# A one-core GNN layer: two batches' h kept on chip, sums of blocks reordered, and where the first gate operands lie

## The chip, the core and the metric

The kernel runs on one core of a Trainium2 chip. A core has five engines that run at the same time and meet only at semaphores: TensorE (PE) for matrix products, VectorE (DVE) and GpSimd (POOL) for elementwise work, ScalarE (ACT) for activations and copies, and SyncE (SP), which here only issues transfers. Each engine takes its instructions strictly in the order of its own queue. SBUF is the on-chip memory (128 partitions), PSUM the eight banks that matmuls write, HBM the memory outside. The metric is the device time of one launch in microseconds (us). The kernel before has a median of 1826.45 us over 3 runs (1825.56 to 1828.58).

## The reference, cut to what matters

There are 32 batches of 512 nodes with 256 features, all in float32. The steps that matter:

```python
h   = relu(layernorm(x))
c   = relu(bn1(conv1x1(h)))                     # then a convolution over 17 neighbouring nodes
x_conv = relu(bn2(conv17(c)) + h)
s   = h @ w_se.T + b_se                         # 3 numbers per node
A   = exp(-|s_i - s_j|^2) * adj                 # 512 x 512 per batch
msg = relu(h @ w_msg.T + b_msg)
x_nmp = A @ msg
gi  = [x_conv, x_nmp] @ w_ih.T + b_ih           # GRU gates, three of 256 each
gh  = h @ w_hh.T + b_hh
r, z = sigmoid(gi_r + gh_r), sigmoid(gi_z + gh_z)
n   = tanh(gi_n + r * gh_n)
out = x + (1 - z) * n + z * h
```

## The kernel before, in words

The batches are worked in two groups of 16 (g = 0 and g = 1), each group in two stages, and a last stage makes the gates for all 32. In time the stages are: first part of group 0 (0 to 157 us of the profile), node loop of group 0 (157 to 446), first part of group 1 (446 to 563), node loop of group 1 (563 to 853), gates of 16 pairs of batches (853 to 1825).

**First part** (`first_part`, L881 to L993). For each batch x is normalised, transposed to h with features on the partitions (tile `hT`, two buffers), stored to HBM (`hd`), put through the 1x1 convolution, and taken to the frequency domain in windows of nodes (tile `xf`). The 17-tap convolution is a product per frequency there. `conv1` (L318) drops its batch's `hT` at its end (L331), except for the last batch of a group. Near the end the first part prepares the node loop: `by_chunks` (L424) copies an `hT` into another order of nodes (tile `hq`, two buffers), and `load_h` (L413) brings back an h from HBM.

**Node loop** (`nodes`, L1036). Its order of batches is the list `todo`: the group's last batch, then the others from the first on. Each turn i works on several batches at once: `message` (PE, then DVE and ACT) of batch i+2 from its `hq`, `factors` and `exponents` of batch i+1 (small transposes on PE, copied out by ACT as `sl` and `sr`, then the products `pd` and the exponentials A), `turn` and `masked` of batch i+1 (DVE transposes the adjacency block and multiplies), and the aggregation A @ msg of batch i. Between these lie the frequency products `multiply(u)` (`product`, L372): unit u has three complex-product terms, the third of which needs `wsum` and `both`, sums that POOL makes two units ahead (`prepare`, L362). 36 units in group 0 (40 in group 1) are spread over the turns, two or three in each.

The aggregation of most batches is done with seven products of half size instead of eight (`aggregate7`, L529). It needs sums of blocks of msg (`ms`) and of A (`ts`), four of each, some of them in place. POOL makes them one turn ahead (`message_sums` L508, `affinity_sums` L499). The last two batches of group 1 are aggregated plainly (`aggregate`, L517). In `aggregate7` ACT copies each finished product out of PSUM (L545 to L553), DVE adds (L554 to L560), and `save_nmp` (L562) stores the result to HBM from ACT's queue. The result tile `nmp` has one buffer.

What orders the work is the program text: the stages run under a manual schedule, so every engine's queue follows the order of the calls. Tiles come from pools; a pool that opens later lies over the memory of one that has closed, and the first writer of a tile waits until the last user of what lay there is done. The pool `nodes` holds adj, msg, A, ts, ms and p7; `first` and `sums` lie over it in the first part of group 1; `sw`, `ops` and `late` in the gate stage.

**Gates** (the block with `load_pair(0)`, from L1164). For each pair of batches there are three operand tiles (`hp`, `np`, `cp`, for h, the aggregation and the convolution), four blocks each, with four more blocks made by POOL (`sums`, L640). The gate products follow the same seven-product scheme, with combined weights in one tile `sw` (seven slices; `load_combined` loads slices 0 and 1 first, the others later). `load_pair(0)` and both weight loads are issued from POOL's queue, so they lie in line with POOL's sums. `gates_rz` (L672) uses the slices in the order 0, 1, 2 and on.

Of the kernel before, what the change touches and what calls it, by code (L numbers as in the profile page):

```python
# [11 lines left out]
FP = mybir.dt.float32  # L12
AF = mybir.ActivationFunctionType
ALU = mybir.AluOpType

P = 128
# [49 lines left out]
def gnn_layer(  # L66
# [251 lines left out]
    def conv1(b):  # L318
        H1[b] = pools["first"].tile([P, NC, D], FP, tag="h1", name=f"h1_{b}", bufs=2)
        h = N // D  # L320
        for c0 in range(0, NC, h):
            p = bank(f"pc1_{b}_{c0}").rearrange("p (c d) -> p c d", d=D)
            for j in range(h):
                c = c0 + j
                for ic in range(DC):
                    nc.tensor.matmul(p[:, j, :], HT[b][:, ic, c * P : (c + 1) * P], w1[:, ic, :],  # L326
                                     start=(ic == 0), stop=(ic == DC - 1))
            h1 = H1[b][:, c0 : c0 + h, :]
            nc.vector.tensor_add(h1, p, shift1_row[:, None, :].to_broadcast([P, h, D]))
            nc.scalar.activation(h1, h1, AF.Relu)  # L330
        if b % GB != GB - 1:  # L331
            del HT[b]

    def windows_to_freq(b, xf):
# [89 lines left out]
    def by_chunks(b):  # L424
        HQ[b] = work.tile([P, DC, N], FP, tag="hq", name=f"hq_{b}", bufs=2)
        for ic in range(DC):
            nc.scalar.copy(chunks(HQ[b][:, ic, :]), by_chunk(HT[b][:, ic, :]))  # L427
        del HT[b]
# [69 lines left out]

    def affinity_sums(b):  # L499
        b11, b12, b21, b22 = quads(A[b], H)  # L500
        t = TS[b] = pools["nodes"].tile([P, 3, 2, H], FP, tag="ts", name=f"ts_{b}", bufs=1)
        sub = ALU.subtract
        nc.gpsimd.tensor_tensor(t[:, 0], b22, b12, op=sub)
        nc.gpsimd.tensor_tensor(b12, b12, b11, op=sub)
        nc.gpsimd.tensor_tensor(t[:, 1], b22, b12, op=sub)
        nc.gpsimd.tensor_tensor(t[:, 2], b21, t[:, 1], op=sub)

    def message_sums(b):  # L508
        a11, a21, a12, a22 = quads(MSG[b], P)
        t = MS[b] = pools["nodes"].tile([P, 3, 2, P], FP, tag="ms", name=f"ms_{b}", bufs=1)  # L510
        sub = ALU.subtract
        nc.gpsimd.tensor_tensor(t[:, 0], a11, a21, op=sub)
        nc.gpsimd.tensor_tensor(a21, a21, a22, op=ALU.add)
        nc.gpsimd.tensor_tensor(t[:, 1], a21, a11, op=sub)
        nc.gpsimd.tensor_tensor(t[:, 2], a12, t[:, 1], op=sub)

    def aggregate(b, dcs=range(2)):  # L517
        if 0 in dcs:
# [10 lines left out]
    def aggregate7(b):  # L529

        m11, s1, m12, m22 = quads(MSG.pop(b), P)
        b11, t1, b21, b22 = quads(A.pop(b), H)
        (s3, s2, s4), (t3, t2, t4) = ([t[:, n] for n in range(3)] for t in (MS.pop(b), TS.pop(b)))
        nmp = NMP[b] = work.tile([P, DC, N], FP, tag="nmp", name=f"nmp_{b}", bufs=1)
        c11, c12, c21, c22 = (nmp[:, i, H * j : H * (j + 1)] for i in range(2) for j in range(2))
        p1 = pools["nodes"].tile([P, H], FP, tag="p7", name=f"p7_{b}", bufs=2)

        def add_product(bk, left, right, first):
            for k in range(2):
                nc.tensor.matmul(bk, left[:, k, :], right[:, k, :], start=(first and k == 0), stop=(k == 1),  # L540
                                 skip_group_check=True)

        x, y, z = (bank(f"pn{k}_{b}")[:, :H] for k in range(3))
        add_product(x, m11, b11, True)
        nc.scalar.copy(p1, x)  # L545
        add_product(y, s2, t2, True)
        nc.scalar.copy(c12, y)
        add_product(z, s1, t1, True)
        nc.scalar.copy(c21, z)
        add_product(x, m12, b21, False)  # L550
        nc.scalar.copy(c11, x)
        add_product(y, s3, t3, False)
        nc.scalar.copy(c22, y)  # L553
        nc.vector.tensor_add(c12, c12, p1)  # L554
        nc.vector.tensor_add(c22, c22, p1)
        nc.vector.tensor_add(c22, c22, c21)
        add_product(z, s4, b22, False)
# [323 lines left out]
    def first_part(g, freq, between, left=()):  # L881
# [39 lines left out]
        for b in range(b0, b1):  # L921
# [18 lines left out]
            if g == 0:  # L940
# [11 lines left out]
                if b == b0 + 2:  # L952
                    slot()
                if b == b1 - 1:
                    load_h(b0)
                if b + 2 < b1:
                    statistics(b + 2)
# [21 lines left out]
            one, two = between(b - b0)  # L979
            conv1(b)  # L980
            if b == b1 - 1:
                load_h(b0)
            for step in one:
                step()
# [2 lines left out]
                step()  # L987
        if g > 0:
            by_chunks(b1 - 1)
            load_h(b0 + 1)  # L990
        windows_to_freq(b1 - 1, xf)
        by_chunks(b0)
        return xf  # L993

    @contextmanager
# [6 lines left out]
    with tc.tile_pool(name="freq", bufs=1) as fpool:  # L1002
# [33 lines left out]
        def nodes(g, xf, units, last, following=()):  # L1036
# [26 lines left out]
            load_h(todo[3])  # L1063
            message(todo[0])
            features(todo[0])
            message_sums(todo[0])
            message(todo[1], [0])
            factors(todo[0])
            message(todo[1], [1])
# [8 lines left out]
            affinity_sums(todo[0])  # L1078
            for i, b in enumerate(todo):
                mine = spread(units, i, last) if i < last else []  # L1080
                more = todo[i + 1 : i + 5]
# [52 lines left out]
        with phase("pw", "ahead"):  # L1134
            with phase("nodes"):
                with tc.manual_schedule():
                    nodes(0, xf, range(UNITS - LEFT), GB, range(UNITS - LEFT, UNITS - LEFT + 2))
            with phase("first", "sums"):
# [20 lines left out]
            with phase("nodes"):  # L1159
# [5 lines left out]
    with phase("late"), phase("sw"), phase("ops", bufs=2), phase("work"), tc.manual_schedule():  # L1165
# [72 lines left out]
```

## Time and profile before

| stage (us of the span) | length | PE busy | DVE busy | ACT busy | POOL busy | mean DMA |
|---|---|---|---|---|---|---|
| 0 to 220 | 220.0 | 211.3 | 165.4 | 117.5 | 89.3 | 265 GB/s |
| 245 to 440 | 195.0 | 190.8 | 164.8 | 88.3 | 157.8 | 215 GB/s |
| 440 to 560 | 120.0 | 119.1 | 98.5 | 47.9 | 44.5 | 232 GB/s |
| 590 to 810 | 220.0 | 220.0 | 172.5 | 100.2 | 168.7 | 236 GB/s |
| 840 to 880 | 40.0 | 36.3 | 8.1 | 10.2 | 29.6 | 257 GB/s |
| 905 to 1745 | 840.0 | 840.0 | 498.4 | 193.3 | 224.3 | 92 GB/s |

The table is from the view of busy time by stage. PE is busy nearly everywhere, so time can be lost in two ways only: in gaps between its instructions, and in instructions that take longer than their like elsewhere. Both are seen in the timeline of PE, where each row is a run of equal instructions with its start, its length, and in brackets the idle time before it and what ended it.

### The profile page before, as it was taken

Reading aid. Unit: us, or ns where it says so; the run is one execution under the profiler, and the core shown is the slowest. Engines: PE = TensorE matmul, PEld = TensorE weight load, DVE = VectorE, ACT = ScalarE, POOL = GpSimd, SP = SyncE. Lnnn points to the kernel's source line nnn. Section 1 sums busy time; section 2 is a strip of 40 time slices with the busy share of each in tenths; the row PEclk is TensorE's granted clock in tenths of the full one; section 3 lists DMA queues with packets and bytes.
Section 4 is the critical chain, followed back from the end, with each engine's and each line's share of the span. In section 5 each row is a group of like instructions: output and inputs, shape, how many; then the busy total and the mean of one; then the engine's idle time right before and its main releaser. Section 6 shows DMA issues by size and latency. Waiting matters only on the chain.

```text
span 1825.0 us, 21270 instructions
## 1 busy us (share of the span) xinstructions
PE 1796.4 (98%) x6974; PEld 1152.0 (63%) x6974; DVE 1236.8 (68%) x2370; ACT 621.9 (34%) x1252; POOL 782.6 (43%) x731
## 2 busy tenths in 40 slices
PE   9999999998999999999999999999999999999998
PEld 6776888887898888886445554555445554555444
DVE  7885788886896787884266556664666466645666
ACT  4555454442345454443212221222212221222121
POOL 3432688777433877776321232223221323133221
PEclk9999999999999999999999999999999999999999
DMA  9989888865669887879142244224422443234412
GB/s 260 309 291 233 234 231 224 238 208 179 214 225 224 250 241 224 244 210 287 50 117 70 57 121 121 87 35 121 121 87 41 116 121 100 54 89 121 116 22 53
DMA packets 308657, 289.32 MB, mean 159 GB/s; under 512 B 148076, under 2 KB 238732, under 8 KB 308164
## 3 DMA queue, kind: packets, MB, share of 16 engines
q1 hardware_dynamic: 282964, 225.79, 46.4%
q10 hardware_dynamic: 18992, 38.68, 6.1%
q0 software_dynamic: 6592, 23.50, 4.1%
q8 instruction: 55, 0.90, 0.2%
q14 instruction: 54, 0.44, 0.1%
HBM read 191.50 MB, written 96.40 MB: 158 GB/s over the span
## 4 chain that ended last, share of the span: by engine, by line
PE 71%; POOL 1%; issue 1%; DMA 1%; DVE 1%; ACT 0%; DVEq 0%; POOLq 0%; ACTq 0%
PE pg L666 29%; PE pn L666 15%; PE py L390 6%; PE pn L540 5%; PE pc L654 5%; PE pm L442 3%; PE pc L326 3%; PE px L341 2%; PE phT L310 1%; PE pd L486 1%; PE pz L666 1%; DMA sw<-ws 1%; DMA nd<-nmp 0%; PE psr L468 0%; POOL hp L644 0%
## 5 line engine op out<-in xcount | busy, mean ns | idle before, releaser
L644 POOL TENSOR_TENSOR hp<-hp 128x512 f32<-128x512 f32 x64 | 80.4, 1267 | 413.6 <-DMA hp<-hd 293.0
L666 PE MATMUL pg<-cp,sw 128*128 128x512 f32 x434 | 223.0, 595 | 2.2 <-DMA sw<-ws 2.2
L666 PE MATMUL pg<-hp,sw 128*128 128x512 f32 x434 | 222.7, 595 | 0.7 <-DVE rz L685 0.5
L666 PE MATMUL pg<-np,sw 128*128 128x512 f32 x434 | 222.6, 594 | 0.6 <-DMA sw<-ws 0.6
L644 POOL TENSOR_TENSOR cp<-cp 128x512 f32<-128x512 f32 x64 | 80.4, 1268 | 227.0 <-ACT cp L660 225.7
L681 ACT ACTIVATE rz<-rz,brz 128x512 f32<-128x512 f32 x93 | 67.0, 721 | 260.2 <-DVE rz L685 260.2
L390 PE MATMUL py<-wt,xf 128*128 128x256 f32 x640 | 154.2, 384 | 0.0
L666 PEld LDWEIGHTS pg<-cp,sw 128*128 128x128 f32 x434 | 82.9, 191 | 106.9 <-issue 103.6
L666 PEld LDWEIGHTS pg<-np,sw 128*128 128x128 f32 x434 | 82.7, 191 | 105.3 <-issue 103.9
L666 PEld LDWEIGHTS pg<-hp,sw 128*128 128x128 f32 x434 | 82.5, 191 | 105.5 <-issue 98.8
L357 POOL TENSOR_TENSOR wsum<-wt 128x512 f32<-128x512 f32 x78 | 105.0, 1347 | 102.1 <-DMA wt<-wd 62.3
L390 PEld LDWEIGHTS py<-wt,xf 128*128 128x128 f32 x640 | 117.1, 190 | 34.9 <-issue 20.5
L805 ACT ACTIVATE nt<-nt,vech 128x512 f32<-128x512 f32 x64 | 46.2, 722 | 236.5 <-DVE nt L804 236.5
L442 PE MATMUL pm<-wmsg,hq 128*128 128x259 f32 x512 | 117.8, 382 | 3.8 <-ACT hq L427 3.8
L326 PE MATMUL pc<-w,hT 128*128 128x256 f32 x512 | 117.9, 383 | 0.8 <-DVE hT L314 0.8
L492 DVE TENSOR_TENSOR A<-A,at 128x512 f32<-128x512 f32 x128 | 109.9, 896 | 6.8 <-ACT A L488 6.8
L666 PE MATMUL pn<-hp,sw 128*128 128x512 f32 x224 | 114.4, 592 | 0.0
L666 PE MATMUL pn<-cp,sw 128*128 128x512 f32 x224 | 114.4, 592 | 0.0
L666 PE MATMUL pn<-np,sw 128*128 128x512 f32 x224 | 114.4, 592 | 0.0
L326 PEld LDWEIGHTS pc<-w,hT 128*128 128x128 f32 x512 | 94.6, 190 | 24.0 <-issue 6.4
L442 PEld LDWEIGHTS pm<-wmsg,hq 128*128 128x128 f32 x512 | 96.3, 189 | 19.4 <-ACT hq L427 4.8
L654 PEld LDWEIGHTS pc<-back,yt 128*128 128x128 f32 x640 | 92.7, 190 | 7.7 <-issue 7.7
(169 smaller groups left out, 3422.0 us busy)
## 6 DMA issues: line engine op xcount, KB each, us to landing
wt<-wd SPq DMA_DIRECT2D x160, 256.0 KB, 5.3
adj<-in_adj_dram SPq DMA_DIRECT2D x128, 256.0 KB, 6.9
wd<-wst SPq DMA_DIRECT2D x64, 320.0 KB, 5.7
yd<-y ACTq DMA_DIRECT2D x80, 256.0 KB, 4.5
yt<-yd SPq DMA_DIRECT2D x30, 640.0 KB, 7.5
hd<-hT SPq DMA_DIRECT2D x32, 512.0 KB, 5.0
nd<-nmp ACTq DMA_DIRECT2D x32, 512.0 KB, 4.8
xb<-in_x_dram SPq DMA_DIRECT2D x128, 128.0 KB, 3.8
```

Of the source, the lines that this page charges most:

```text
L326: nc.tensor.matmul(p[:, j, :], HT[b][:, ic, c * P : (c + 1) * P], w1[:, ic, :], start=(ic == 0), stop=(ic == DC - 1))
L341: nc.tensor.matmul(p[:, j * 2 * L : (j + 1) * 2 * L], H1[b][:, c0 + j, ic * P : (ic + 1) * P], fwd, start=True, stop=True)
L357: nc.gpsimd.tensor_tensor(t, WT[g, u][:, 0], WT[g, u][:, 1], op=ALU.add)
L390: nc.tensor.matmul(dst, v[:, ic, :], w[:, ic, :], start=(ic == 0), stop=(ic == DC - 1))
L442: nc.tensor.matmul(p[:, : D + NS], hq[:, ic, c * P : (c + 1) * P], wmsg[:, ic, :], start=(ic == 0), stop=(ic == DC - 1))
L492: nc.vector.tensor_mul(A[b][:, mc, :], A[b][:, mc, :], AT.pop((b, mc)))
L540: nc.tensor.matmul(bk, left[:, k, :], right[:, k, :], start=(first and k == 0), stop=(k == 1), skip_group_check=True)
L644: nc.gpsimd.tensor_tensor(t[:, dst, :], t[:, a, :], t[:, b, :], op=sub)
L654: nc.tensor.matmul(bk[:, t0:t1], YT[p][j][:, c, oc * P : (oc + 1) * P], back[:, n : n + t1 - t0], start=(c == 0), stop=(c == len(spans) - ...
L666: nc.tensor.matmul(bk[:, t], sw[:, k, q, o, :], terms[k][q][:, t], start=(first and i == 0), stop=(i == len(ks) - 1), skip_group_check=True)
L681: nc.scalar.activation(rz[:, g, j, :], src, AF.Sigmoid, bias=brz[:, g : g + 1], scale=1.0)
L805: nc.scalar.activation(n, n, AF.Tanh, bias=b_in[:, i : i + 1], scale=1.0)
```

## The change

It has several parts.

- The h of a group's last *two* batches stays on chip: `conv1` keeps their `hT`, `by_chunks` of the last but one is done in the last turn of the first part, and `todo` begins with both. One `load_h` from HBM (512 KB) at the head of each node loop falls away, and the copy that went with it.
- In a turn, `by_chunks` for a later batch moves from before the aggregation to behind it, and the store of the aggregated batch is issued at once behind it, no longer with the next turn's first stores. On ACT's queue the store now stands ahead of the copies `sl` and `sr` of the next turn.
- The block sums of msg and A are interleaved in the order in which the products use them, and in `aggregate7` the product of s1 and t1 comes second instead of third.
- In group 0's last turn the third frequency unit moves from before the aggregation to behind it.
- `ts`, `ms` and `p7` (three buffers instead of two) get a pool of their own, `seven`, which lies in front of `nodes`. In the gate stage the tile `np` of the first pair then lies over those tiles; before, it lay over `adj`.
- The load of weight slices 2 to 6 is issued before the sums of the first `np` instead of behind them.

The purpose is to take waits out at the stage boundaries. No arithmetic is added or removed.

```diff
@@ conv1
-        if b % GB != GB - 1:
+        if b % GB < GB - 2:
             del HT[b]
@@ affinity_sums, message_sums
-        t = TS[b] = pools["nodes"].tile([P, 3, 2, H], FP, tag="ts", name=f"ts_{b}", bufs=1)
+        t = TS[b] = pools["seven"].tile([P, 3, 2, H], FP, tag="ts", name=f"ts_{b}", bufs=1)
...
+    def block_sums(b):
+        m, a = message_sums(b), affinity_sums(b)
+        for step in (*m[:2], *a[:2], m[2], a[2], m[3], a[3]):
+            step()
@@ aggregate7
-        p1 = pools["nodes"].tile([P, H], FP, tag="p7", name=f"p7_{b}", bufs=2)
+        p1 = pools["seven"].tile([P, H], FP, tag="p7", name=f"p7_{b}", bufs=3)
...
         nc.scalar.copy(p1, x)
+        add_product(z, s1, t1, True)
+        nc.scalar.copy(c21, z)
         add_product(y, s2, t2, True)
         nc.scalar.copy(c12, y)
-        add_product(z, s1, t1, True)
-        nc.scalar.copy(c21, z)
@@ first_part, last batch of a group (both groups)
+                    by_chunks(b - 1)
                     load_h(b0)
...
                     by_chunks(b)
-                    load_h(b0 + 1)
...
         windows_to_freq(b1 - 1, xf)
-        by_chunks(b0)
@@ nodes
-            todo = [b1 - 1] + list(range(g * GB, b1 - 1))
+            todo = [b1 - 1, b1 - 2] + list(range(g * GB, b1 - 2))
...
                     exponents(more[0])
-                    if len(more) > 2:
-                        by_chunks(more[2])
                     masked(more[0], [0, 1])
-                for u in mine[1:2] if more else mine[1:]:
+                for u in mine[1:2]:
                     multiply(u)
...
                 flush()
-                stores.append(partial(save_nmp, b))
+                if len(more) > 2:
+                    by_chunks(more[2])
+                save_nmp(b)
                 if more and i + 1 <= last:
-                    message_sums(more[0])
-                    affinity_sums(more[0])
-                if more:
-                    for u in mine[2:]:
-                        multiply(u)
+                    block_sums(more[0])
+                for u in mine[2:]:
+                    multiply(u)
@@ pools of both node loops
-            with phase("nodes"):
+            with phase("seven", "nodes"):
@@ head of the gate stage
         sums(HP[0], True)
+        load_combined(sw, 2, 7)
         sums(NP[0], False)
-        load_combined(sw, 2, 7)
```

More of the change, by code (lines that the diff above doesn't have):

```diff
@@ L500, in affinity_sums @@
         b11, b12, b21, b22 = quads(A[b], H)
-        t = TS[b] = pools["nodes"].tile([P, 3, 2, H], FP, tag="ts", name=f"ts_{b}", bufs=1)
+        t = TS[b] = pools["seven"].tile([P, 3, 2, H], FP, tag="ts", name=f"ts_{b}", bufs=1)
         sub = ALU.subtract
[L503 to L506, printed above, removed]
+        return [partial(nc.gpsimd.tensor_tensor, dst, x, y, op=sub)
+                for dst, x, y in ((t[:, 0], b22, b12), (b12, b12, b11), (t[:, 1], b22, b12), (t[:, 2], b21, t[:, 1]))]
     def message_sums(b):
         a11, a21, a12, a22 = quads(MSG[b], P)
-        t = MS[b] = pools["nodes"].tile([P, 3, 2, P], FP, tag="ms", name=f"ms_{b}", bufs=1)
+        t = MS[b] = pools["seven"].tile([P, 3, 2, P], FP, tag="ms", name=f"ms_{b}", bufs=1)
         sub = ALU.subtract
[L512 to L515, printed above, removed]
+        return [partial(nc.gpsimd.tensor_tensor, dst, x, y, op=op)
+                for dst, x, y, op in ((t[:, 0], a11, a21, sub), (a21, a21, a22, ALU.add),
+                                      (t[:, 1], a21, a11, sub), (t[:, 2], a12, t[:, 1], sub))]
+    def block_sums(b):
+        m, a = message_sums(b), affinity_sums(b)
+        for step in (*m[:2], *a[:2], m[2], a[2], m[3], a[3]):
+            step()
     def aggregate(b, dcs=range(2)):
@@ L981, in first_part @@
             if b == b1 - 1:
+                by_chunks(b - 1)
                 load_h(b0)
@@ L989, in first_part @@
             by_chunks(b1 - 1)
-            load_h(b0 + 1)
         windows_to_freq(b1 - 1, xf)
-        by_chunks(b0)
         return xf
@@ L1065, in nodes @@
             features(todo[0])
-            message_sums(todo[0])
+            for step in message_sums(todo[0]):
+                step()
             message(todo[1], [0])
@@ L1077, in nodes @@
             prepare(pw, g, units[1], xf)
-            affinity_sums(todo[0])
+            for step in affinity_sums(todo[0]):
+                step()
             for i, b in enumerate(todo):
@@ L1158, in gnn_layer @@
                     xf = first_part(1, freq_tile, between, left)
-            with phase("nodes"):
+            with phase("seven", "nodes"):
                 with tc.manual_schedule():
```

## The prediction

> **What bounds the kernel now.** I read the page first, then the waits of PE, then PE's timeline around each wait, and last the queues of the engine that ended it. The page says that PE has no room left but its gaps:
>
> ```profile
> PE 1796.4 (98%) x6974; PEld 1152.0 (63%) x6974; DVE 1236.8 (68%) x2370; ACT 621.9 (34%) x1252; POOL 782.6 (43%) x731
> ```
>
> The span is 1825.0 us, so PE sits idle for 28.6. PE's waits, longest total first (total, times, longest):
>
> ```profile
> PE py L390 <- POOL both L370: 4.4, 2, 4.2
> PE pm L442 <- ACT hq L427: 3.8, 2, 1.9
> PE pg L666 <- DMA sw<-ws: 2.8, 2, 2.2
> PE pn L540 <- ACT p L545: 2.8, 1, 2.8
> ```
>
> Each long one sits at a stage boundary. The node loops between them (590 to 810: PE 220.0 of 220.0) and the gates (905 to 1745: 840.0 of 840.0) have no gap, so a change there buys nothing unless it adds a wait. PE's timeline, start of the first node loop:
>
> ```profile
> 180.17 1.03 PE L540 MATMUL pn<-A,msg 128*128 128x256 f32 x4
> 183.96 2.07 PE L540 MATMUL pn<-A,msg 128*128 128x256 f32 x4 [2.77 <-ACT p L545]
> ```
>
> The like group takes 1.03 before the gap and 2.07 after it: a gap also slows what follows. ACT's timeline shows why p was late; it stood in line behind a copy that waited for a load:
>
> ```profile
> 181.95 1.14 ACT L427 COPY hq<-hT 128x512 f32<-128x512 f32 x2 [3.02 <-DMA hT<-hd]
> 183.54 0.37 ACT L545 COPY p<-pn 128x256 f32<-128x256 f32 x1
> ```
>
> End of that loop, PE and then POOL:
>
> ```profile
> 430.74 1.89 PE L390 MATMUL py<-wt,xf 128*128 128x256 f32 x8
> 436.82 2.08 PE L390 MATMUL py<-wsum,both 128*128 128x256 f32 x4 [4.19 <-POOL both L370]
> 446.39 1.64 PE L310 MATMUL phT<-ident,xn 128*128 128x128 f32 x8 [0.93 <-DVE xn L302]
> ...
> 436.04 0.72 POOL L370 TENSOR_TENSOR both<-xf 128x256 f32<-128x256 f32 x1
> ```
>
> Start of the gates, PE and then POOL:
>
> ```profile
> 869.21 1.02 PE L666 MATMUL pg<-hp,sw 128*128 128x512 f32 x2
> 874.16 2.07 PE L666 MATMUL pg<-cp,sw 128*128 128x512 f32 x2 [2.21 <-DMA sw<-ws]
> ...
> 847.68 1.47 POOL L621 DMA_DIRECT2D np<-nd  x2 [16.45 <-DVE at L475]
> 861.07 1.61 POOL L608 DMA_DIRECT2D sw<-ws  x3
> ```
>
> POOL's queue is held for 16.45 us by the np load, which waits until adj, below it in memory, has been read. Everything behind it on POOL (sums of hp and np, then the second half of sw) starts late.
>
> Last, ACT around the batch before the last, for the wait that the change adds:
>
> ```profile
> 412.75 0.59 ACT L470 COPY sr<-psr 128x512 f32<-128x512 f32 x1 [0.17 <-PE psr L468]
> 416.12 0.33 ACTq L563 DMA_DIRECT2D nd<-nmp  x1
> ```
>
> **What the Trainium skill says.** "TensorE: Matmul & The Clock Gate", section "What's actually happening": the PE clock is halved after an idle window of about 3.4 us and comes back after as much steady work, and the window runs freely. The trace agrees on the halving (granted clock 0.55, 0.50 and 0.81 in the three stretches of 3 us from 873 on), but here gaps of 0.59 and 2.21 with one slow group between them are enough. "SBUF — State Buffer", section "Who interferes with whom": a DVE instruction with two SBUF inputs contends with GpSimd's reads. The trace agrees: L555 takes 0.42 at 835.15 with POOL idle, 0.96 at 413.55 beside POOL's sums. "DMA: Bandwidth & Descriptors", section "Queues, rings and completion order": each DMA engine goes round between the queues with work. From 840 to 843.7 two queues share the engines (SP's 0.93 MB, ACT's 0.52 MB), which fits.
>
> **The change part by part.**
>
> *Start of group 0's loop.* The seven products run from 178.44 to 189.12, 10.68 us; the same 28 instructions take 6.04 in the chain of waits elsewhere: 4.64 lost. With the copy of hq moved behind L553 on ACT, p no longer waits for the load, and this wait is gone. The dropped load takes 512 KB off a saturated stretch (DMA share 0.97 to 1.24 from 156 to 183): at about 240 GB/s 2.1 us. adj of the first batch now lies over memory that PE leaves before 157, so DVE starts its transposes up to 3 us earlier than at 168.53, frees the PSUM banks of pm earlier, and the group pd at 173.52 (2.30 long against 1.14) may regain 1.2. Against it stands the next turn: POOL's sums start at 191.2, since wsum waits for a wt load issued at 182.91. If PE comes 5 us earlier, the sums must too; of the 8.7 us of sums the interleaved order has those of the second and third product ready 4.3 and 6.5 us after the start. By the 2 to 3 us that the loads come earlier this just holds. I take 5.0, from 3.0 to 5.8. The wait of 1.9 for hq (168.01, and 574.24 in group 1) stays: that copy is still queued behind the same four exponents. In group 1 no wait of the first kind exists: 0.
>
> *End of group 0's loop.* From 430.74 to the next unit's product at 447.88 PE takes 17.14. Its work there: 12 product instructions 2.59 + aggregation 6.04 + transposes 0.87 = 9.50. So 7.64 are lost. With the aggregation first, POOL's sums (429.56 to 434.9) are in time: the second product needs its in-place sum, the fourth of eight from 426.12, by 431.6, ready about 430.5; the third needs the sixth, ready 432.6, a wait of 0.2. `both` is there at 436.76, when the seven products end. Gain 7.4. The x load of group 1's second batch now waits for p7 (until 437) instead of starting at 432.60; its statistics come on DVE some 6 us later, so it costs nothing.
>
> *A new wait, one turn earlier.* The store of nmp now stands ahead of sl and sr on ACT, and waits for DVE's last add L560 (415.64 + 0.41 = 416.05). Queued behind it: sl, sr, two y copies, exponents; for sr waits PE's pd. In usual turns pd comes 6.7 us after the aggregation (257.90 to 264.64), and sr would be ready 4.5 after it: the store 3.3 behind (261.21), its issue 0.33, then sl and sr back to back 0.8 (168.34 to 169.13). No cost. In the turn before the last there is no message work, and pd follows after 3.1 us, at 415.24. sr would be ready at 416.12 + 0.33 + 0.8 = 417.3: a gap of 2.1. pd itself was stretched to 1.66 by banks that are free then, so 1.6 net, plus some half-clock: 2.0, from 0.5 to 4.5. Net gain of this end: 7.4 - 2.0 = 5.4 (3 to 7).
>
> *Head of the gates.* np now lies over ms, ts and p7, which L560 releases at 836.9. POOL then issues np at 837.0 and the first part of sw to about 840, does the hp sums (4 x 1.27 = 5.2) to 845.3, and issues the rest of sw at about 845.3 instead of 861.07. The transfers from 826 on are 14.64 MB; at the 360 GB/s of full stretches 40.7 us, and the late ones (np of pair 1 and x, 2.1 MB) are behind, so sw lands near 862, before PE needs it at 869. From 869.21 to 880.65 PE does six products that elsewhere take 36.05 / 42 = 0.858 each: 11.44 - 5.15 = 6.29 regained. Against it: the earlier np and sw join the store of nd at 837.10, on which ACT waits 6.15 and through it the last aggregation (PE gaps 0.50 and 0.41 at 845.62 and 848.01). A third queue on the engines makes its transfer 1 to 1.5 us longer: minus 1.1 (0 to 3). Net 5.2 (3 to 6.3).
>
> *The rest at nothing.* The order of products and sums in the steady turns: POOL is done 3 us before PE asks (810.72 against 813.68). The later hq copy: on ACT it would end near 257.9, 3 us before its products at 261.04. The third p buffer: no wait for it seen. The copy of the last-but-one batch in the first part: ACT has gaps of 1.6 and 1.1 us there, and is 40% busy.
>
> Sum: 5.0 + 5.4 + 5.2 = 15.6. 1826.45 - 15.6 = 1810.9.
>
> **The rivals.**
> - *All gaps close, no new wait:* 5.8 + 7.4 + 6.3 + 0.9 (the two small gaps) = 20.4, 1806. For it: the new waits hang on DVE and DMA timing of a few tenths. Against it: L560 at 416.05 is plain in the trace. 0.13.
> - *One boundary stays as it is* because loads bind there: the start of the first loop is full of DMA, and if its loads come no earlier, POOL's sums hold the next turn. About 15.6 - 7 = 8.6 gained, 1818. For it: DMA share over 1; against it: 512 KB fewer. 0.16.
> - *Nothing left:* the nd store ahead of sr and the shared transfers give the gain back, 1826. 0.04.
> - *Slower:* store before sr binds in the usual turns too. There it has 2.1 us of slack; if DVE lagged 3 more in all 28 turns, 28 x 0.9 = 25 lost against 15.6, 1836. Against it: DVE is 78% busy in the loops and gets no work more. 0.05.
>
> **How the numbers follow.** The main case has 0.62: 1811, between 1807 and 1815. The bound of 0.2% is 3.65 us, so main, best and middle rival are all faster: 0.92 with a little of the tail; same 0.04; slower 0.04. The range takes the best and the middle rival: 1804.5 to 1819.
>
> **What would show it.** Right: no PE wait on p L545, both L370 or sw; phT of group 1 some 10 us earlier than 446.39; the rest of sw issued near 845; the wait on hq still twice 1.9; one new wait of pd on sr near 410. Wrong: PE waits in the middle of the node loops, waits on POOL's ts in the second turn, or a wait for A of more than 3 us near 845.

## The result, and the profile after

The changed kernel takes 1844.03 us, the median of 4 runs (1843.07 to 1847.82); the kernel before takes 1826.01 in the same session (1823.36 to 1828.58). The ratio is 1.0103 with an interval of 1.0082 to 1.0123. The change costs 18 us where a gain of 15.6 was forecast.

The page of the changed kernel, PE's line and the costliest wait of POOL (busy time and mean ns of one, then idle time before it and what ended most of it):

```profile
PE 1804.6 (98%) x6974; PEld 1157.9 (63%) x6974; DVE 1240.2 (67%) x2370; ACT 622.0 (34%) x1252; POOL 776.0 (42%) x731
...
L357 POOL TENSOR_TENSOR wsum<-wt 128x512 f32<-128x512 f32 x78 | 102.6, 1315 | 130.9 <-DMA wt<-wd 112.7
```

The span is 1842.2, so PE is idle for 37.6 (28.6 before) and busy for 8.2 more with the same 6974 instructions: half of the loss is gaps, half is slower or stalled groups. POOL's sum `wsum` waits 112.7 for weights; before it was 62.3. PE's waits (total, times, longest):

```profile
PE pm L442 <- ACT hq L427: 3.9, 2, 1.9
PE psl L463 <- DVE fl L456: 3.8, 2, 3.1
PE py L390 <- POOL both L370: 3.7, 2, 2.7
PE pd L486 <- ACT sr L470: 3.0, 1, 3.0
PE pn L542 <- POOL A L517: 2.7, 1, 2.7
PE pn L525 <- DVE A L492: 2.7, 3, 1.3
```

The waits on p and on sw are gone, as forecast, and so is the long one on `both` at the end of group 0 (the two here are in group 1). In their place stand waits that were not there: on `fl`, on `both` in group 1, on POOL's A.

**Where the time went.** PE's timeline has one group `pd` (L486) in each turn, 0 to 15 in group 0 and 16 to 31 in group 1. The stretch from one such mark to another, taken in both traces, gives the ledger; for instance pd 2 to pd 3 is 195.86 to 212.41 before, 16.55, and 194.46 to 218.14 after, 23.68, so +7.13. "Last px" is the last group of 16 instructions `px`. The last two columns are the mended kernel and the kernel with two edits, which come below.

| stretch | before | changed | forecast | mended | two edits |
|---|---|---|---|---|---|
| start to pd 1 | 173.52 | +4.39 | 0 | +1.30 | +1.38 |
| pd 1 to 2, first seven products | 22.34 | -5.79 | -5.0 | -5.79 | +0.06 |
| pd 2 to 3, second turn | 16.55 | +7.13 | 0 | +2.16 | 0.00 |
| pd 3 to 14, usual turns of group 0 | 189.79 | +4.47 | 0 | +0.21 | 0.00 |
| pd 14 to 15, turn before the last | 13.04 | +3.11 | +2.0 | 0.00 | 0.00 |
| pd 15 to phT of group 1, end of group 0 | 31.15 | -4.44 | -7.4 | -6.72 | -4.93 |
| phT to last px, first part of group 1 | 106.45 | +0.23 | 0 | -0.76 | -0.92 |
| last px to pd 17, head of group 1's loop | 26.91 | +6.86 | 0 | +0.29 | +1.68 |
| pd 17 to 19, second and third turn there | 38.36 | +5.97 | 0 | +4.50 | -0.08 |
| pd 19 to 31, usual turns of group 1 | 222.24 | -0.43 | 0 | -0.19 | +0.01 |
| pd 31 to the inverse | 12.91 | +2.06 | +1.1 | +0.47 | +0.13 |
| inverse to PE's end | 963.57 | -6.29 | -6.3 | -6.02 | -6.29 |
| sum | | +17.3 | -15.6 | -10.6 | -9.0 |

The three gains are there, in about the size forecast (that at the end of group 0 once the half clock, PE's slower clock after a gap, that follows the new wait is taken away, below). They are outweighed by seven losses, five of them in stretches that the forecast had at nothing. Two traces below run the code of the kernel before unchanged up to the end of group 0; there start to pd 1 is +1.54 and +1.38, and pd 1 to pd 2 is -4.44 and +0.06. So these two stretches vary by themselves, and what the change does there is read with that in mind.

**The second turn of group 0.** PE, SP, ACT and POOL of the changed kernel:

```profile
201.95 1.25 PE L542 MATMUL pn<-A,msg 128*128 128x256 f32 x4 [2.70 <-POOL A L517]
204.40 2.08 PE L542 MATMUL pn<-ts,ms 128*128 128x256 f32 x4 [1.20 <-POOL ts L517]
206.27 1.91 PE L542 MATMUL pn<-A,msg 128*128 128x256 f32 x4
...
188.36 0.34 SPq L415 DMA_DIRECT2D hT<-hd  x1
188.80 2.54 SPq L353 DMA_DIRECT2D wt<-wd  x4
...
186.26 0.81 ACTq L1053 DMA_DIRECT2D yd<-y  x2
...
195.04 1.31 POOL L357 TENSOR_TENSOR wsum<-wt 128x512 f32<-128x512 f32 x1 [15.08 <-DMA wt<-wd]
```

PE waits for POOL's sums, which stand behind `wsum`, which waits for weights that SP issues at 188.80 (182.91 before; the loop itself starts 4.4 later), because the load of hT ahead of them is issued at 188.36. Among SP's waits of 176 to 190 us that load has the longest:

```profile
SPq L415 <- DMA yd<-y: 9.8, 1, 9.8
```

It waits for a *store*, of product y of unit 0, issued from ACT's queue at 186.26. The two have no data in common. The program as built gives the transfers of SP and ACT eight completion semaphores in turn, and a transfer is issued only when the one that last had its semaphore is complete. From the list of waits in the programs:

```
kernel    transfer on SP                    last holder of its semaphore
before    hT load of turn 0, group 0        the hT load before it (SP L415)
changed   hT load of turn 0, group 0        store of y of unit 0 (ACT L1053)
before    weights of unit 3, group 1        an adj load (SP L411)
changed   weights of unit 3, group 1        store of y of unit 0 (ACT L1053)
```

That store is held back until the aggregation has been issued, so ACT issues it behind the copies of the seven products. In group 1 it is the weights of unit 3 themselves that wait: SP issues them at 606.14, behind ACT's stores of 604.05.

**The head of group 1's loop.** DVE, SP and ACT:

```profile
578.03 0.16 DVE L444 TENSOR_TENSOR st<-pm,bmsg 128x3 f32<-128x3 f32 x1 [9.57 <-DMA ws<-w]
...
570.17 0.32 SPq L415 DMA_DIRECT2D hT<-hd  x1
570.59 0.38 SPq L987 DMA_DIRECT2D ws<-w  x1
...
569.03 1.12 ACT L427 COPY hq<-hT 128x512 f32<-128x512 f32 x2
```

With the tiles of the seven products in front, msg and st lie 12,288 bytes further on. The first one written, st, then lies over the last combined weights, and these are still being stored. The store is late because it stands on SP behind the hT load, which waits for the copy of the kept batch to hq.

**The turn before the last of group 0**, ACT and PE:

```profile
427.38 0.33 ACTq L565 DMA_DIRECT2D nd<-nmp  x1
427.74 0.27 ACT L465 COPY sl<-psl 128x128 f32<-128x128 f32 x1 [6.69 <-DVE nmp L562]
427.91 0.59 ACT L470 COPY sr<-psr 128x512 f32<-128x512 f32 x1
...
428.55 2.09 PE L486 MATMUL pd<-sr,sl 9*128 9x512 f32 x8 [3.04 <-ACT sr L470]
430.57 3.78 PE L390 MATMUL py<-wt,xf 128*128 128x256 f32 x8
```

The forecast wait is there, 3.04 long, and the groups after it run at half clock (8 product instructions take 3.78, elsewhere 1.89). The store itself waits for DVE's last add, and two of the adds ahead of it take longer than the 0.96 and 0.84 of the kernel before:

```profile
423.74 1.49 DVE L557 TENSOR_TENSOR nmp<-nmp,p 128x256 f32<-128x256 f32 x1
425.27 1.37 DVE L558 TENSOR_TENSOR nmp<-nmp 128x256 f32<-128x256 f32 x1
```

They are 1.06 longer together, and 1.06 on the gap of 2.1 that was forecast is 3.1.

**The head of the gates**, POOL:

```profile
858.97 1.47 POOL L623 DMA_DIRECT2D np<-nd  x2 [6.87 <-DVE nmp L562]
...
867.22 1.61 POOL L610 DMA_DIRECT2D sw<-ws  x3
```

The trace is 21.9 behind here, so these are the 837.0 and 845.3 of the forecast. No wait on sw is left.

### The profile page after: what moved, and what is told of

The parts are those of the page before. It is cut to its first block, busy times and chain, and to the rows that moved or that the text cites. A ratio compares the mean times of both kernels' runs of the same rounds, so it can differ in the third digit from the quotient of the medians.

```text
span 1842.2 us, 21281 instructions
## 1 busy us (share of the span) xinstructions
PE 1804.6 (98%) x6974; PEld 1157.9 (63%) x6974; DVE 1240.2 (67%) x2370; ACT 622.0 (34%) x1252; POOL 776.0 (42%) x731
## 4 chain that ended last, share of the span: by engine, by line
PE 89%; DVE 3%; DMA 3%; issue 2%; POOL 2%; ACT 1%; SPq 0%; ACTq 0%; DVEq 0%; POOLq 0%
PE pg L668 30%; PE pn L668 15%; PE py L390 10%; PE pn L542 9%; PE pm L442 5%; PE pc L326 5%; PE pc L656 5%; PE px L341 3%; PE pd L486 2%; PE pw L254 2%; PE phT L310 1%; PE pz L668 1%; PE psr L468 1%; DMA wt<-wd 1%; POOL ts L517 0%
## 5 line engine op out<-in xcount | busy, mean ns | idle before, releaser
L357 POOL TENSOR_TENSOR wsum<-wt 128x512 f32<-128x512 f32 x78 | 102.6, 1315 | 130.9 <-DMA wt<-wd 112.7
L442 PE MATMUL pm<-wmsg,hq 128*128 128x259 f32 x512 | 124.2, 396 | 4.2 <-ACT hq L427 3.9
L442 PEld LDWEIGHTS pm<-wmsg,hq 128*128 128x128 f32 x512 | 100.1, 197 | 22.0 <-ACT hq L427 4.8
```

Source lines behind the costliest of these rows:

```text
L357: nc.gpsimd.tensor_tensor(t, WT[g, u][:, 0], WT[g, u][:, 1], op=ALU.add)
L442: nc.tensor.matmul(p[:, : D + NS], hq[:, ic, c * P : (c + 1) * P], wmsg[:, ic, :], start=(ic == 0), stop=(ic == DC - 1))
```

## The experiments

All ratios are to the kernel before in the same session, whose median is 1827.99 for the last two, 1828.52 for unit 0's store, the store of nmp, the store of the combined weights and the tiles behind the node loop, and 1828.50 for the other four. The steps of the traces are measured against the one trace of the kernel before above, whose span is 1825.0 in a run of 1826.73, 1 to 2 below these medians. A traced run can itself lie 2.7 us off its kernel's median, so steps and ratios need not agree to a few us.

**Store of unit 0's product at once.**

```diff
-                product(pw, g, u, xf, stores)
+                product(pw, g, u, xf, stores if u > 0 else None)
```

> The changed kernel, but the store of unit 0's product y is issued as soon as y is written (in both node loops) and not held back until the aggregation has been issued. Everything else stays. Theory A (shared completion semaphores): the load of hT on SP in group 0's first turn waits for the completion of this store, because both have the same one of eight DMA semaphores, and in group 1 the load of unit 3's weights waits for it in the same way; all loads behind them on SP start late, POOL's sums start late, and PE waits in the second and third turn. Then the hT load is issued near 180 and not at 188.36, unit 3's weights near 599 and not at 606.14, the step from the second pd group of the loop to the third is again 16.5 us in group 0 (changed kernel 23.7), and the three waits of PE at 609 to 624 go: 7.1 + about 6 = 13 us less, near 1831. Rival B (the DMA engines are full there, the semaphore is not what binds): the loads come no earlier, 0 to 3 us less, 1841 to 1844. Rival C (the copy of hq moved behind the aggregation holds the hT buffer): the hT load is still issued right after that copy, near 188: 0 to 6 us less.

Measured: 1829.33, ratio 1.0007 (0.9996 to 1.0018). ACT issues the store at 177.05, and SP no longer stands:

```profile
179.44 1.81 SPq L415 DMA_DIRECT2D hT<-hd  x1
183.06 8.08 SPq L353 DMA_DIRECT2D wt<-wd  x4
```

The second turn of group 0 is at -0.01 (changed kernel +7.13), pd 17 to 19 at -0.09 (+5.97); unit 3's weights go at 589.48 (606.14 in the changed kernel). That is 13.2 from one store in each loop, in group 0 issued some eight microseconds earlier, with every load, tile and copy as in the changed kernel. Theory A holds, to the tenth in its steps (it put unit 3's weights near 599; those at 599.79 are unit 4's); B and C fall, since the DMA engines take the earlier loads and the copy of hq was not touched.

**Store of nmp behind sl and sr.**

```diff
-                save_nmp(b)
+                stores.append(partial(save_nmp, b))
```

> The changed kernel, but the store of nmp goes back into the list that is emptied later, behind sl and sr of the next batch on ACT. Theory A (ACT waits for DVE's last add before it can copy sr and y, in the usual turns too): both the wait of pd for sr near 428 (3.0 us, and about 3.2 more of half-clock groups after it) and the slow drift of 4.5 us over the two-unit turns from 250 to 412, where the pd groups take up to 2.0 us and not 1.14, go away: 10 us less, near 1834. Rival B (the drift comes from the new order of POOL's sums, which run beside DVE's adds): only the wait near 428 goes, 6 us less, near 1838, and the pd groups stay long.

Measured: 1837.96, ratio 1.0043 (1.0029 to 1.0057). pd 14 to 15 is at 0.00, the end of group 0 at -7.35. The usual turns of group 0 drift by 2.42 instead of 4.47. So the store explains the wait and all that follows it, 3.1 + 2.9 = 6.0, and half of the drift. The timeline suggests how: y's copies stand behind it on ACT too, and DVE needs them before it can empty the banks of pm (in the turn at 304.82 DVE idles 1.80 for y in the changed kernel, 1.19 at the like place before). The other half has another cause. Neither expectation was right about the drift, and the time is that of rival B.

**Block sums in the old order**, on top of the edit above.

```diff
-        for step in (*m[:2], *a[:2], m[2], a[2], m[3], a[3]):
+        for step in (*m, *a):
```

> As the run with the store of nmp behind sr, and besides this POOL's eight block sums in the order of the kernel before: the four of the message first, then the four of A. The run with the store alone still drifts by 2.4 us from the fifth to the fourteenth pd group (156.5 against 154.1 of the kernel before); there DVE's adds L557 and L558 take 1.49 and 1.38, in the kernel before 0.95 and 0.84. Theory A (a DVE add with two inputs in SBUF waits for the POOL instruction that runs beside it; in the order of use the long sums of A, 1.27 each, run beside the adds, in blocks the short ones of the message, 0.73): the adds are at 0.95 and 0.84 again, the stretch takes 154.1 to 154.6, about 2 us less. Against it the last aggregation of group 0 may wait for its second product, up to 2 us more, so the whole is 1.001 to 1.0045 of the kernel before. Rival B (the drift comes from the later copy of hq on ACT): the stretch stays at 156 to 157.

Measured: 1839.91, ratio 1.0055 (1.0039 to 1.0071), above the range that was expected. But the drift is at 0.41. DVE's groups of 250 to 400 us, for the run before this one and then for this one (last numbers: busy us, mean ns of one, idle before):

```profile
L557 DVE TENSOR_TENSOR nmp<-nmp,p 128x256 f32<-128x256 f32 x9 | 10.7, 1190 | 0.0
L558 DVE TENSOR_TENSOR nmp<-nmp 128x256 f32<-128x256 f32 x8 | 10.5, 1310 | 0.3
```

```profile
L557 DVE TENSOR_TENSOR nmp<-nmp,p 128x256 f32<-128x256 f32 x8 | 6.5, 810 | 0.0
L558 DVE TENSOR_TENSOR nmp<-nmp 128x256 f32<-128x256 f32 x8 | 6.3, 786 | 0.3
```

These are means over turns in which POOL's sums fall beside the adds and turns in which they do not. In one turn where they do, first in the order of use and then in blocks, with the sum of POOL that runs beside the add:

```profile
366.31 1.49 DVE L557 TENSOR_TENSOR nmp<-nmp,p 128x256 f32<-128x256 f32 x1
366.07 1.45 POOL L517 TENSOR_TENSOR ts<-A 128x512 f32<-128x512 f32 x1
...
367.36 0.94 DVE L557 TENSOR_TENSOR nmp<-nmp,p 128x256 f32<-128x256 f32 x1
367.23 0.79 POOL L517 TENSOR_TENSOR msg<-msg 128x256 f32<-128x256 f32 x1
```

Beside a sum of A the two adds take 1.49 and 1.38, beside a sum of msg 0.94 and 0.83, and 0.41 where POOL does not run beside them; L560 and L562, which have one input in PSUM, take 0.41 in both orders. This is what the Trainium skill, "SBUF — State Buffer", section "Who interferes with whom", says of a DVE instruction with two SBUF inputs, and the trace adds the price: the add pays by the length of the POOL instruction beside it. The time is nevertheless no better than without this edit, because in two turns the sums are late in this order: a wait of 5.03 for POOL's A in the second turn, whose loads are late anyway (2.8 in the run before), and of 0.45 in the last, where the end of group 0 gives 5.85 instead of 7.35. In this trace the start up to pd 1 is 2.2 later as well, which no edit explains. So the order of use is right for the last turn and wrong for the usual ones.

**Store of the combined weights ahead of the hT load.**

```diff
             if b == b1 - 1:
                 by_chunks(b - 1)
-                load_h(b0)
             for step in one:
                 step()
+            if b == b1 - 1:
+                load_h(b0)
```

> The changed kernel, but in the last batch of group 1's first part the load of hT is issued behind that stage's combined-weight steps, so that the store of the last combined weights stands ahead of it on SP. Theory A: the first message of group 1 is written over memory that this store still reads; the store is issued at 570.59 only because it stands behind the hT load, which waits for the copy of the kept batch to hq (done at 570). With the store issued near 565, DVE starts on the first message near 573 and not at 578.03, and PE reaches the second pd group of the loop 5 us earlier: 4 to 5.5 us less, near 1839. Rival B (DVE waits for something else, for instance for PE or for adj): no change of DVE's start beyond 0.5 us, 1844.

Measured: 1836.73, ratio 1.0050 (1.0034 to 1.0067). The store is issued at 560.96, and DVE's first instruction of the loop waits for PE alone:

```profile
570.34 0.16 DVE L444 TENSOR_TENSOR st<-pm,bmsg 128x3 f32<-128x3 f32 x1 [4.88 <-PE pm L442]
```

Last px to pd 17 is at +0.30 (changed kernel +6.86; the four other traces with st over this store and the store late have 9.0 to 9.3). Theory A holds, with 6.6 instead of 4 to 5.5: the slow groups pm after the wait (3.39 and 5.36 in the changed kernel, 1.92 and 3.85 before) go too. pd 17 to 19 stays at +7.49, as it should if that has its own cause.

**Tiles of the seven products behind those of the node loop.**

```diff
-            with phase("seven", "nodes"):
+            with phase("nodes", "seven"):
```

(in both loops)

> The changed kernel, but the tiles of the seven products are placed behind those of the node loop and not ahead of them, so that adj, msg and st lie at the addresses of the kernel before. Theory A (the waits of DVE before the first message, 7.0 us at 160.68 and 9.57 at 578.03, come from where msg and st now lie): both go; about 3 us less in group 0 and 5.5 to 7 in group 1. At the head of the gates np lies over adj again, so its load waits for the last transposes as in the kernel before and the second part of sw is issued near 855 + offset, 6 us later than in the changed kernel: 0 to 3 us more there. Net 6 to 9 less, near 1836. Rival B (DVE's waits have another cause, the new order of the loads): they stay, and only the loss at the gates shows, 1844 to 1847.

Measured: 1835.42, ratio 1.0035 (1.0021 to 1.0049). Last px to pd 17 is at +0.30 as in the run before, though the weights' store is again issued at 569.69 behind the hT load: it takes both, a late store and st over it. At the head of the gates np is issued at 861.61 after 17.06 of waiting for `at`, and yet inverse to end is at -5.42, only 0.9 short. And pd 31 to the inverse is at -0.21 instead of +2.06. So the early load of np brings less than it costs.

**The order of sw alone**, in the kernel before.

```diff
         sums(HP[0], True)
+        load_combined(sw, 2, 7)
         sums(NP[0], False)
-        load_combined(sw, 2, 7)
```

> The kernel before with one edit: the second part of sw is issued ahead of the sums of np, the tiles stay where they are. The prediction gave the whole gain at the head of the gates (6.3) to np lying over the tiles of the seven products; the run with these tiles behind lost only 0.9 of it. Theory A (the order on POOL's queue is enough): sw's second part is issued near 855 instead of 861.07, PE's stretch 869.21 to 880.65 (11.44 for six products of 0.86) shortens to 5.2 to 6.1: 5.3 to 6.3 less, ratio 0.9966 to 0.997. Rival B (np must be issued early): sw lands 5 us earlier but still late, 2 to 3 us less, ratio 0.9985.

Measured: 1820.94, ratio 0.9960 (0.9944 to 0.9975). The second part of sw goes at 853.76 (861.07 before), inverse to end is at -6.30: all of the gain of the changed kernel, without any tile moved. In this trace pd 1 to 2, which is unchanged code, is 4.44 shorter, and its run is the fastest of the four; the median is 7.6 below the kernel before, 1.3 more than the head explains.

**Copy of hq ahead of the masks again**, in the changed kernel.

```diff
                     exponents(more[0])
+                    if len(more) > 2:
+                        by_chunks(more[2])
                     masked(more[0], [0, 1])
...
-                if len(more) > 2:
-                    by_chunks(more[2])
                 save_nmp(b)
```

> The changed kernel, with the copy of hq of the batch three ahead back ahead of the masks, where the kernel before has it. Prediction's step: this copy waits for the load of hT, p of the first seven products stands behind it on ACT, and PE waits for p. Theory A: the wait of about 2.8 on p and the slow groups after it come back (the step from the second to the third pd group is 22.3 in the kernel before and 16.55 in the changed one: 20 to 22 here), while the semaphores are dealt out as in the kernel before, so that neither the hT load nor unit 3's weights wait for unit 0's store: the 7.1 us of the second turn of group 0 and the 6 of group 1 go. Net 13 - 5 = 8 less, 1834 to 1837, ratio about 1.005. Rival B (with one load of h fewer hT lands before the copy asks): no wait on p, 13 less, ratio about 1.002. Rival C (the late loads do not come from the semaphores): second turn still 23, ratio 1.010 or more.

Measured: 1830.16, ratio 1.0007 (0.9998 to 1.0016). Rival B: there is no wait on p here, pd 1 to 2 is at -5.79 as in the changed kernel; one load of h fewer is enough. The semaphores are dealt as in the kernel before, and with that the second turn of group 0 is at -0.01 and pd 17 to 19 at -0.08. Two different edits, one that moves the store and one that changes what shares with it, take away the same 13 us. The usual turns of group 0 drift by 2.60 here instead of 4.47, though the store of nmp and the order of the sums are those of the changed kernel: beside these two, the later copy of hq on ACT has a part in the drift. With both mended its place no longer counts (0.21 with the copy late, 0.36 with it early, in the two mended kernels below).

**The mended kernel.** The changed kernel with unit 0's store at once, the store of nmp behind sr, the order of use for the sums of each loop's last turn only, and the tiles of the seven products behind.

```diff
-    def block_sums(b):
+    def block_sums(b, last):
...
-        for step in (*m[:2], *a[:2], m[2], a[2], m[3], a[3]):
+        for step in (*m[:2], *a[:2], m[2], a[2], m[3], a[3]) if last else (*m, *a):
...
-                product(pw, g, u, xf, stores)
+                product(pw, g, u, xf, stores if u > 0 else None)
...
-                save_nmp(b)
+                stores.append(partial(save_nmp, b))
...
-                    block_sums(more[0])
+                    block_sums(more[0], len(more) == 1)
...
-            with phase("seven", "nodes"):
+            with phase("nodes", "seven"):
```

> The changed kernel mended in all points found: unit 0's store at once, store of nmp behind sr, sums of the message ahead of those of A but for the last turn of each loop, tiles of the seven products behind those of the node loop. It keeps the two h on chip, the third unit behind the aggregation, the later hq copy and the earlier load of sw. Against the kernel before, from the runs so far: first turns -3.5, second turn 0, steady turns 0 to +0.5, end of group 0 -7.4, between the loops +0.5 to 1, start of group 1 0 to +2, head of the gates -5.4: 13 to 16 less, ratio 0.9915 to 0.993. Rival: the parts do not add up because the DMA engines bind at the two starts: one of the second turns stays 5 to 7 us long, ratio 0.996.

Measured: 1816.82, ratio 0.9937 (0.9925 to 0.9949): faster than both kernels, by 11.7 against the kernel before, where 13 to 16 were expected. The column of the ledger shows the rest: pd 17 to 19 is still at +4.50. In this program another pair meets: an adj load of group 1 has the semaphore of unit 0's store, SP's issue of those four loads takes from 570.22 to 579.08, and unit 3's weights follow at 579.72.

**The same with the copy of hq early instead of the store at once.**

```diff
-                product(pw, g, u, xf, stores if u > 0 else None)
+                product(pw, g, u, xf, stores)
...
                     exponents(more[0])
+                    if len(more) > 2:
+                        by_chunks(more[2])
...
-                if len(more) > 2:
-                    by_chunks(more[2])
                 stores.append(partial(save_nmp, b))
```

> The mended kernel in another form: the copy of hq goes back ahead of the masks instead of the early store of unit 0; store of nmp behind sr, sums of the message first but for the last turn, tiles of the seven products behind those of the node loop stay. In the mended kernel the semaphores put the second adj load of group 1 behind unit 0's store (SP waits from 571 to 578) and the second and third turn there lose 4.7. Theory A (which loads share a semaphore with which stores is what sets the second turns, and the place of the hq copy decides it here): in this form neither an adj load, an hT load nor unit 3's weights share with unit 0's store in either group; the start of group 1 is as in the kernel before (0 lost), the rest as in the mended kernel: 15 to 17 less than the kernel before, ratio 0.9905 to 0.992. Rival B (group 1's loss in the mended kernel comes from the DMA engines): still 4 to 5 lost there, ratio 0.993 to 0.995.

Measured: 1812.69, ratio 0.9916 (0.9900 to 0.9932), the lowest of all, though its interval meets those of the mended kernel and of the two edits below, and within what theory A gave. The second turn of group 0 is at 0.00. pd 17 to 19 is at +2.98 where theory A gave 0, so the shared semaphore was a part of the 4.50 only. Of the rest 1.0 is a longer group pd (2.18 at 569.36, before 1.14), and a wait of 1.75 for `both` stays at 594.36. Why its weights are late there is left open; rival B, the DMA engines, is not excluded for this rest. pd 1 to 2 is at -4.25 with a wait of 1.28 on p: the early copy can still be in the way of p, by that much.

**Two edits in the kernel before:** sw's order as above, and the third unit behind the aggregation in the last turn.

```diff
-                for u in mine[1:2] if more else mine[1:]:
+                for u in mine[1:2]:
...
-                if more:
-                    for u in mine[2:]:
-                        multiply(u)
+                for u in mine[2:]:
+                    multiply(u)
```

> The kernel before with two edits alone: the third unit of the last turn of group 0 behind the aggregation, and the second part of sw ahead of the sums of np. Prediction's steps: 7.4 at the end of group 0 and 6.3 at the head of the gates. The order of sums and products is the old one here: the second product needs the seventh of the eight sums and not the fourth. POOL's sums end at 434.9 and the aggregation starts at 430.7: a wait of 1 to 2 us with some half clock after it. Theory A (the order of sums and products is worth this much in the last turn): 4 to 6 less at the end of group 0, with a wait of pn on POOL's ts there; with the head 10 to 12 less, ratio 0.9935 to 0.9945. Rival B (it is worth nothing, since PE comes later than reckoned): 7.4 less there, ratio 0.9925.

Measured: 1815.63, ratio 0.9929 (0.9907 to 0.9950). The end of group 0 gives 4.93 with this wait in the old order of sums:

```profile
435.02 1.13 PE L540 MATMUL pn<-ts,ms 128*128 128x256 f32 x4 [1.80 <-POOL ts L505]
```

So the order of use is worth 7.35 - 4.93 = 2.4 in that one turn (1.5 by the run with the sums in blocks): theory A. The head gives 6.29. Two moves of a few lines bring as much as the mended change, and nothing else in the ledger moves by more than 1.7.

## Why the prediction was wrong

- **Start of group 0, first seven products (5.0): right in place and nearly in size**, 5.79, the step that ends at the floor of 16.55. The reason was half right: p was late because of the load, but the later copy of hq was not needed for it, one load fewer did nearly all (early copy: no wait in one run, 1.28 in the other). How much is gained is less certain than the 5.79: of the three traces of the kernel's own code up to there two take 22.3 to 22.4 and one 17.90.
- **Second turn of group 0 (0): this is the first step that failed.** It said of POOL's sums "By the 2 to 3 us that the loads come earlier this just holds." The weights came six microseconds *later* (issued at 188.80 instead of 182.91), 4.4 of them because the loop started later. The forecast looked at bytes and at the DMA share, and took for granted that SP would go on issuing. It had read SP's queue for what waits for buffers, and not for which earlier transfer must be complete before a load can be issued. Cost 7.1. One of its own signs of being wrong came, a wait on POOL's ts in the second turn (1.20). The rival "One boundary stays as it is" had the place and the size, 7, but for another cause, full DMA engines; with the same loads and an earlier store the loss is gone.
- **The usual turns (0): wrong by 4.5.** It checked that POOL is done in time, which is true, and that sr has 2.1 us of slack. Two things were missed: the y copies too stand behind the store on ACT, and DVE's emptying of the pm banks waits for them (2.0, by the store's run); and the order of the sums sets how long DVE's adds take beside them (2.0, by the run with sums in blocks). The later copy of hq has a part in it too (2.60 with the copy early); the shares overlap. The slower rival had this mechanism for the store and gave it 0.05.
- **A new wait in the turn before the last (2.0): right in place, too small.** The wait is 3.04, since the adds that the store waits for are themselves slowed by 1.06; and it gave "some half-clock" a few tenths where 2.9 came. Together 6.0, outside the 0.5 to 4.5 given.
- **End of group 0 (7.4): right**, 7.35 once the half clock is away (6.7 in the two mended kernels). 1.5 to 2.4 of it come from the order of the sums.
- **Start of group 1 (0): the second step that failed**, 12.8. The forecast asked only whether the old wait on p exists there. It did not ask what lies under the tiles that the new pool pushes on (6.9 in this trace, weights still being stored, late because the kept batch's copy holds SP), nor, again, about the semaphores (6.0). It had used the same kind of overlap for np, and to the good, and looked for it in one place only.
- **Last aggregations (1.1): right in kind**, 2.06.
- **Head of the gates (6.3): right in size and in every time on POOL, wrong in the cause**, so the size is in part luck. The order of two lines on POOL's queue gives all of it; np over the seven tiles gives nothing more and costs the 2.06 of the point before.
- **The four unexplained microseconds up to pd 1** are partly no effect: unchanged code shows +1.4 and +1.5 there. DVE waits 7.0 for the stores of the frequency weights, over which st now lies, but in the run with unit 0's store at once it waits 7.2 for PE at the same place. Of the six traces with that layout three lose nothing between pd 0 and pd 1 and three 1.7 to 2.9; one with the old layout loses 1.6. What decides it is left open.

Sum of the misses: 7.1 + 4.5 + 4.0 + 12.8 + 1.0 = 29.4, less 0.8 gained more at the first products, and 4.4 at the start: 33.0, and the distance from -15.6 to +17.3 is 32.9.

## What to carry to other kernels

When a change moves a transfer or drops one, list for each load on the issuing queue what it waits for, completion semaphores included: a store on another queue can hold a load that has nothing to do with it, and everything behind it. When a tile pool is added in front of another, ask for each tile pushed on what lies under it and when the last reader is done, not only for the one that is meant to gain. And try the few-line reorderings of a queue before the memory plan: here two of them brought as much as the mended change.

## What the runs showed of the hardware

- An add on DVE with two inputs in SBUF takes 0.41 to 0.42 with POOL idle, 0.83 to 0.96 beside POOL's sums of msg (0.73 alone) and 1.37 to 1.50 beside its sums of A (1.27 alone). POOL's own are stretched as well, to 0.79 and 1.45 in the lines above. So the length of POOL's instructions sets DVE's time, not only their number.
- The same gap does not cost the same. A wait of 3.04 at pd 15 is followed by groups of 2.09 and 3.78 in the changed kernel and of 1.16 and 3.61 in the run with the early hq copy (1.14 and 1.89 elsewhere), so there the half clock comes one group later. A gap of 2.70 and one of 1.20 with a short group between them brought half clock (granted clock 0.50 from 203 to 209), a gap of 2.71 at 623.70 none. The Trainium skill, "TensorE: Matmul & The Clock Gate", section "What's actually happening", says that the window for this runs freely, which would give such differences; no run here tests it. Gaps of 2.7 to 3.1 cost between nothing and 3 us each here.
- Traces of unchanged code differ by up to 4.5 us in one stretch (pd 1 to 2), where loads and copies race. A step of a few microseconds at such a place should be read from more than one trace.
